# The slot-table reads on GpSimd's queue, and another order for the first half of an attention step

## The chip, the cores and the metric

The kernel runs on one core of one Trainium2 chip. The metric is the device time of one execution in microseconds (us). The engines of the core run side by side, each through its own list of instructions in order: TensorE (PE) multiplies matrices, VectorE (DVE) and ScalarE (ACT) work element by element, GpSimd (POOL) does the same and issues indirect transfers, SyncE (SP) here only issues transfers.

## The reference

The input x is 8 batches x 1024 tokens x 512 channels. Two blocks follow each other, each behind a layer norm and with a residual sum:

```python
theta_q = xh / (1.0 + jnp.abs(w_q)) + b_q + t * phi_q      # theta_k alike, theta_v without t
Q = jnp.concatenate([cos_q, sin_q], axis=-1)               # K alike; V = cos_v + sin_v
scores = jnp.einsum('bqhd,bkhd->bhqk', Q, K) / scale       # 16 heads, 32 + 32 features, causal
out = jnp.einsum('bhqk,bkhd->bqhd', softmax(scores), V)
x = x + cos_o + sin_o                                      # of theta_out = out / (1 + |w_out|) + b_out
...
probs = softmax(x @ Wr + br); topk_p, topk_e = top_k(probs, 2)     # 8 experts, two for each token
buf = rows of x by expert, 160 places for each expert and batch; later tokens are dropped
y = relu(buf @ W1[e] + b1[e]) @ W2[e] + b2[e]                      # 512 -> 2048 -> 512
x = x + sum over both experts of probability * y
```

sin and cos come from a table of 2048 entries with linear interpolation.

## The kernel before, in words

**Attention.** 32 steps, n = 4b + c: batch b, and block c of 128 channels (four heads, two pairs of heads). In one step PE computes, for the first pair, ten tiles of scores (called S1 to S10 here: three for queries 0 to 511, seven for queries 512 to 1023; `scores`, L600 and the mask L614), ACT takes the exponent of each (L620), and PE multiplies each with V (`attend`, L634). The ten products of the first pair are called F1 to F10 here. The second pair has the scores T1 to T10 and products of which only the first three, G1 to G3, are done in the same step; the other seven, R1 to R7, are left for the next step. Products are unlike in width: R7, like F10, has 256 columns, F1 to F3 together have 512 + 512 + 256.

PE's accumulators for scores are three buffers of two banks each (`two_banks`). The same three serve the transposes `turn` (L202, attention output back to tokens), the transposes of `qk_pre`, and the router. A buffer comes free when ACT has taken the exponent, or DVE has copied what it holds.

Between the two halves of a step ACT loads the table of sines, computes the sines for the next step (L514 for the cosine, L433 for the rest) and loads the table of exponents again. DVE multiplies the results (`qk_post`, L436), and eight transfers of SP (L527: four of `qk_c`, four of `qk_r`) rearrange them into the `qk` tiles that the next step's scores read. `qk_f`, `qk_r`, `qk_c` have one buffer each: `qk_pre` of the step after the next writes `qk_r` (L426) only when the L527 transfers have read the old one.

**The order of the work.** On PE, ACT and DVE the order is the order of the program text; it is written out by hand in the loop over n, with generators: `some(k, *gens)` takes k pieces, `with_asides(k)` takes k scores and after each one piece of every side job. The transfers of SP and GpSimd are placed by the tile framework, in an order that it fixes when the program is built; each queue then runs in that order. The first half of a step before the change is, on PE:

R1-R3 | S1-S5 | R4-R6 | S6-S9 | R7 F1 F2 | S10 | `turn` of the step before | F3 | (sines on ACT) F4-F10

and then T1, T2, `turn`, T3-T5, G1-G3, T6-T10, and the transposes of `qk_pre`.

**The router.** When batch b-1 is finished, in the second half of step n = 4b (c = 0), `router` begins: the residual rows go to `out` (L691), then layer norm statistics (L694, L339-L347), normalised rows `xn2` (`rows`, L704) which SP stores for the experts (L710), and four groups of two row tiles. A group has transposes on PE and a copy by DVE to `xT` (`features`, L731; called f0 to f3 here), and logits on PE with copies by DVE to `lg` and `prob` (`sums`, L765, L748, L770, L772; u0 to u4 here, of which u4 only finishes the last group). f0 stands at the end of step c = 0; u0, f1, u1, f2, u2, f3, u3, u4 are dealt out over step c = 1 by `router_step`; the choice of experts follows in c = 2 (`part(route)`), and in c = 3 the slots of the tokens are known. Then `scatter` issues 16 indirect transfers on GpSimd's queue (L682), which write (token, weight) into the batch's slot table in device memory, and `fetch_slots` reads a slot table back into the tile `meta` (L881, two transfers of 8-byte elements, 1280 of them). In the program text of step 4b + 3 the fetch of batch b-2's table stands ahead of the scatters of batch b-1; in SP's queue the framework has put each fetch earlier than that: the reading of a table stands between the `qk_base` load (L476) of the step in which that same table is scattered and the L527 transfers of the step after it.

**Experts.** From L1023 on PE runs the two layers for 8 experts in 16 chunks. `find_rows` and the row gathers L962 need `meta`; the last batch's router runs inside the first chunk (`ending`).

Of the kernel before, what the change touches and what calls it, by code (L numbers as in the profile page):

```python
# [22 lines left out]
B, S, D = 8, 1024, 512  # L23
# [50 lines left out]
def preln_attn_moe_kernel(  # L74
# [21 lines left out]
    nc = tc.nc  # L96
# [404 lines left out]
    def qk_abs(st):  # L501

        f, r = st
        c = qkt.tile([P, 2, S], F32, name="qk_c")
        for i in range(2):
            nc.scalar.activation(c[:, i, :], r[:, i, :], AF.Abs)
            yield c, f, r
        for i in range(2):
            square(f[:, i, :])
            yield c, f, r  # L510
# [26 lines left out]
    def v_pre(n):  # L537

        b, c = divmod(n, NCH)
        t = trig.tile([P, S], F32, name="v_p", bufs=1)  # L540
        p = t.bitcast(I32)
        r = trig.tile([P, S], I32, name="t_r")
        for h in range(2):
            nc.vector.tensor_tensor(
                by_token(t)[:, 4 * h : 4 * h + 4, :],
                xn_tiles[b][h][:, :, c * P : (c + 1) * P], along(inv_v, c, 4), ALU.mult,
            )
        yield p, r
        nc.vector.tensor_tensor(by_token(p), by_token(t), along(bias_v, c), ALU.add)
        yield p, r  # L550
        angle(p, r)
        yield p, r
# [73 lines left out]
    def attend(n, pr, h, es, halves):  # L626

        vt = v_tiles[n % 2]
        av = ps_av.tile([P, 512], F32, name="av")
        tiles = tiles_of(h)  # L630
        for i, parts in enumerate(tiles):
            for kb, q0, w, at in parts:
                for a in range(2):
                    nc.tensor.matmul(  # L634
                        av[a * 64 : (a + 1) * 64, q0 - 512 * h :],
                        lhsT=vt[:, kb, 2 * pr + a, :], rhs=es[i][:, a, at : at + w],
                        start=kb == 0, stop=i + 1 == len(tiles),
                    )
            if i + 1 == len(tiles):
                av_sb = avp.tile([P, 512], F32, name="av_sb")  # L640
                q = 2 * (n % NCH) + pr
                nc.vector.tensor_scalar(av_sb, av, inv_o[:, q : q + 1], None, ALU.mult)
                halves.append(av_sb)
            yield

    def some(count, *gens):

        for gen in gens:
            while count and next(gen, 0) is None:
                count -= 1  # L650

    def rest(gen):
        got = None
        for got in gen:
            pass
        return got
# [207 lines left out]
    def part(gen):  # L864

        for name in gen:
            if name is not None:
                return
            yield

    def keep(box, gen):
        for box[0] in gen:
            yield

    def fetch_slots(b, eng):

        rows = slot_d[b][: E * CAP, :].rearrange("(e c) k -> c e k", e=E)
        s0 = b * CAP
        while s0 < (b + 1) * CAP:
            s1 = min((s0 // P + 1) * P, (b + 1) * CAP)  # L880
            eng.dma_start(  # L881
                meta[s0 % P : s0 % P + s1 - s0, :, s0 // P, :],
                rows[s0 - b * CAP : s1 - b * CAP],
            )
            s0 = s1
# [238 lines left out]
    def experts_begin():  # L1124

        for name, bufs in (("w1p", 3), ("t1p", 2), ("xep", 1), ("tmp_p", 2), ("gp", 2)):
            pools[name] = to_end.pool(name, bufs, **right)
        find_rows(0)
        for k in range(AHEAD):
            load_ahead(k)  # L1130
        yield from start(gather(0), first_parts)
        mix_w1(0, 0)
# [69 lines left out]
    for n in range(NCK):  # L1202
        more, late = n + 1 < NCK, last is not None
        b, c = divmod(n, NCH)
        if n == NCK - 1:
            to_inputs.close()
            first_rows = experts_begin()
        pos_n = trig.tile([P, S], F32, name="o_p")
        if late:
            e11, halves1, pos = last  # L1210
        es, halves = [[], []], [[], []]

        products = [attend(n, 0, h, es[h], halves[0]) for h in range(2)]
        if late:
            products.insert(0, attend(n - 1, 1, 1, e11, halves1))
        ahead = [scores(pairs[0], h, es[h]) for h in range(2)]
        places, v_box = [None], [None]
        absolutes = keep(places, qk_abs(qk_st)) if more else iter(())  # L1220
        asides = [keep(v_box, v_pre(n + 1))] if more else [first_rows]
        if c == 2 and route is not None:
            asides.append(part(route))
        if b == 0 and c in (1, 2):
            asides.append(layernorm1(1, c - 1))
        elif c == 0 and b + 1 < B:
            asides.append(layernorm1(b + 1, 1))
        elif c == 3 and b + 2 < B:
            asides.append(layernorm1(b + 2, 0))

        router_step = lambda: next(route) if c == 1 and route is not None else None

        def with_asides(count):
            for _ in range(count):
                some(1, *ahead)
                for g in asides:
                    next(g, None)

        if late:
            some(3, *products)  # L1240
        router_step()
        if n == 0:
            with_asides(3)
            qk_st = rest(qk_pre(1))
            angle(*qk_st)
            absolutes = keep(places, qk_abs(qk_st))
            with_asides(2)
        else:
            with_asides(5)
        router_step()  # L1250
        some(2, absolutes)
        if late:
            some(3, *products)
        router_step()
        with_asides(4)
        router_step()
        some(2, absolutes)
        if more:
            v_st = v_box[0]
            square(v_st[0])  # L1260
        some(3, *products)
        router_step()
        with_asides(1)
        rest(absolutes)
        for g in asides:
            rest(g)
        if n == 1:
            load_mid(0)
        if late:
            turn(1, halves1, pos)  # L1270
            o_st = o_pre(n - 1, pos)
        router_step()
        if c == 1 and b > 0:
            load_mid(b)
        if n == 2:
            load_b1()
        if c == 2 and b + 2 < B:
            load_x(b + 2)
        if c == 3 and b > 0:
            next(route)  # L1280
            if b > 1:
                fetch_slots(b - 2, nc.sync)
            scatter()


        some(1, *products)
        if more:
            qk_st = places[0]
            qk_sin(qk_st)
            sine(v_st[1])  # L1290
        if late:
            sine(o_st[1])
        if more:
            post = qk_post(qk_st)
            next(post)
        some(NTT, *products)
        if n == 0:
            load_base(2)


        es, halves1 = [[], []], []
        ahead = [scores(pairs[1], h, es[h]) for h in range(2)]
        router_step()
        if c == 2 and route is not None:
            next(route)
        some(2, *ahead)
        turn(0, halves[0], pos_n)
        if more:
            next_pairs = rest(post)
            v_post(n + 1, v_st)  # L1310
        some(3, *ahead)
        if late:
            square(o_st[0])
            o_post(n - 1, o_st)
        some(3, attend(n, 1, 0, es[0], halves1))
        router_step()
        if late and c == 0:
            route = router(b - 1)
            next(route)
        some(5, *ahead)  # L1320
        if n + 2 < NCK:
            qk_st = rest(qk_pre(n + 2))
            angle(*qk_st)
        if late and c == 0:
            next(route)
        if n + 3 < NCK:
            load_base(n + 3)
        last = (es[1], halves1, pos_n)
        pairs = next_pairs if more else None
# [4 lines left out]
    def ending():  # L1334

        o_st = o_pre(NCK - 1, pos_n)
        yield
        sine(o_st[1])
        square(o_st[0])
        for _ in range(3):  # L1340
            yield
        o_post(NCK - 1, o_st)
        for _ in range(3):
            yield
        for name in router(B - 1):

            for _ in range(5 if name == "tiles" else 1):
                yield
        fetch_slots(B - 2, nc.sync)
        scatter()  # L1350
        fetch_slots(B - 1, nc.gpsimd)

    experts(ending())

# [30 lines left out]
```

## Time and profile before

| | us |
|---|---|
| median of 3 runs (lowest, highest) | 3448.29 (3447.84, 3449.66) |
| the profiled execution | 3456.62, its span 3454.9 |
| PE busy / DVE / ACT / POOL in the span | 3239.6 / 2297.2 / 1320.1 / 407.1 |
| first expert product on PE (L1023) starts at | 1430.20 |
| start of the sines (L514), steps 11 to 18 | 531.29, 569.52, 627.91, 667.50, 705.73, 743.96, 801.49, 841.08 |
| mean granted TensorE clock | 0.979 |

The starts of the sines give the length of a step: 38.23 us from one to the next in most places (531.29 to 569.52), 39.6 where the choice of experts runs, and more at the place where the router begins (569.52 to 627.91, 743.96 to 801.49). In a timeline row the columns are start, duration, engine, line, operation, output and inputs, number of instructions merged; the bracket at the end is the idle time before it on that engine and what ended it. A merged group of matmuls is counted to the modelled end of its last one, which overlaps the next group a little, so lengths below are taken from start to start. SPq is SP's queue of transfers: a row there begins when the transfer's waits are over.

### The profile page before, as it was taken

What the parts mean: (1) busy time and instruction counts of PE and PEld (TensorE: products, weight loads), DVE (VectorE), ACT (ScalarE), POOL (GpSimd) and SP (SyncE); (2) the same over time, 40 slices, a digit from 0 to 9 for tenths busy, and PEclk for the clock granted to TensorE, in tenths of its full rate; (3) what the DMA queues carried; (4) which work ended last, traced back from release to release, by engine and by line L of the source; (5) the groups of instructions that cost most, each with busy time, mean ns of one, the idle gap of its engine ahead of it and who ended that gap; (6) DMA issues with size and microseconds to landing.
All of it is one profiled execution on the core that took longest, in us unless ns stands there. A gap on an engine that the chain in (4) does not pass through costs nothing.

```text
span 3454.9 us, 48850 instructions
## 1 busy us (share of the span) xinstructions
PE 3239.6 (94%) x18942; PEld 2177.8 (63%) x18942; DVE 2297.2 (66%) x5064; ACT 1320.1 (38%) x1609; POOL 407.1 (12%) x349
## 2 busy tenths in 40 slices
PE   3999898989898989899999999999999999999998
PEld 1444443444444444468868878778778688688687
DVE  7877777777777767574575576566656746745844
ACT  5777777777777777320111111111101101101201
POOL 1000202020202020331101100100110011011010
PEclk9999999999999999999999999999999999999999
DMA  4534353535263435232322422312322313323321
GB/s 147 142 103 145 90 166 72 165 76 168 73 195 75 147 72 156 68 101 56 113 62 49 113 55 55 107 49 65 109 44 68 107 37 80 101 43 82 95 40 25
DMA packets 242703, 320.79 MB, mean 93 GB/s; under 512 B 30312, under 2 KB 163112, under 8 KB 230056
## 3 DMA queue, kind: packets, MB, share of 16 engines
q1 hardware_dynamic: 220304, 275.54, 27.3%
q0 software_dynamic: 22080, 42.10, 6.8%
q8 instruction: 150, 2.46, 0.3%
q14 instruction: 81, 0.66, 0.1%
q10 hardware_dynamic: 88, 0.02, 0.0%
HBM read 188.67 MB, written 61.82 MB: 73 GB/s over the span
## 4 chain that ended last, share of the span: by engine, by line
PE 74%; ACT 12%; DVE 8%; DMA 3%; issue 2%; SPq 0%; POOL 0%; POOLq 0%; ACTq 0%; DVEq 0%
PE ps_p L1068 28%; PE ps_p L1023 25%; PE ps_s L600 10%; PE av L634 8%; ACT e L620 5%; DMA qk<-qk_r 1%; ACT qk_c L514 1%; ACT qk_f L430 1%; ACT t_r L433 1%; ACT qk_r L433 1%; PE ps_s L202 1%; PE ps_t L979 1%; ACT L620 1%; ACT L514 1%; DVE st_mid L577 1%
## 5 line engine op out<-in xcount | busy, mean ns | idle before, releaser
L620 ACT ACTIVATE e<-ps_s 128x1024 f32<-128x1024 f32 (+1 forms) x640 | 569.4, 937 | 353.3 <-PE ps_s L614 236.4
L600 PE MATMUL ps_s<-qk 64*128 64x512 f32 (+3 forms) x3072 | 612.7, 518 | 67.9 <-ACT e L620 42.2
L1068 PE MATMUL ps_p<-w,hid 128*128 128x256 f32 x2560 | 569.8, 380 | 0.0
L634 PE MATMUL av<-e,v 128*64 128x512 f32 (+3 forms) x3072 | 544.7, 501 | 0.0
L1068 PEld LDWEIGHTS ps_p<-w,hid 128*128 128x128 f32 x2560 | 484.7, 190 | 66.4
L600 PEld LDWEIGHTS ps_s<-qk 64*128 64x128 f32 x3072 | 264.9, 191 | 269.4 <-issue 147.3
L1068 PE MATMUL ps_p<-w_t,hid 128*128 128x256 f32 x1920 | 430.0, 379 | 0.0
L634 PEld LDWEIGHTS av<-e,v 128*64 128x64 f32 x3072 | 205.3, 139 | 320.0 <-issue 305.1
L1068 PEld LDWEIGHTS ps_p<-w_t,hid 128*128 128x128 f32 x1920 | 361.9, 190 | 47.7
L1023 PE MATMUL ps_p<-xe_s,t 128*128 128x256 f32 (+1 forms) x1024 | 299.4, 435 | 5.8 <-DVE t L1008 3.4
L1023 PE MATMUL ps_p<-xe,w 128*128 128x256 f32 (+1 forms) x1024 | 301.2, 437 | 1.3 <-DVE o_p L671 1.2
L1023 PE MATMUL ps_p<-xe,t 128*128 128x256 f32 (+1 forms) x1024 | 296.8, 433 | 0.0
L682 POOL DMA_INDIRECT slot_d<-token,slot x128 | 163.9, 1280 | 1126.8 <-issue 621.6
L1023 PEld LDWEIGHTS ps_p<-xe_s,t 128*128 128x128 f32 x1024 | 194.4, 191 | 90.9 <-DVE t L1008 8.0
L1097 ACT COPY p<-ps_p 128x256 f32<-128x256 f32 x40 | 14.8, 369 | 613.3 <-PE ps_p L1068 613.3
L1023 PEld LDWEIGHTS ps_p<-xe,w 128*128 128x128 f32 x1024 | 194.3, 191 | 84.5 <-DVE hid L1041 5.3
L1023 PEld LDWEIGHTS ps_p<-xe,t 128*128 128x128 f32 x1024 | 194.4, 190 | 80.9 <-issue 0.4
L1090 POOL DMA_INDIRECT out_dram<-y,slots x80 | 126.3, 1578 | 668.2 <-DVE y L1085 531.6
L962 POOL DMA_INDIRECT xg<-xn_d,source x80 | 78.3, 978 | 1053.7 <-PE ps_t L979 1019.2
L1038 ACT ACTIVATE p<-ps_p,b_t 128x256 f32<-128x256 f32 (+1 forms) x128 | 65.5, 511 | 329.7 <-DVE y L1084 169.7
L1042 ACT ACTIVATE hid<-hid 128x256 f32<-128x256 f32 (+1 forms) x128 | 60.1, 470 | 324.6 <-DVE hid L1041 324.6
L1055 ACT ACTIVATE hid<-hid,b_more 128x256 f32<-128x256 f32 (+1 forms) x128 | 71.8, 561 | 277.1 <-DVE hid L1054 277.1
(211 smaller groups left out, 3838.3 us busy)
## 6 DMA issues: line engine op xcount, KB each, us to landing
w<-in_L_ffn_W_dram SPq DMA_DIRECT2D x256, 256.0 KB, 3.3
qk<-qk_c SPq DMA_DIRECT2D x128, 256.0 KB, 4.2
qk<-qk_r SPq DMA_DIRECT2D x128, 256.0 KB, 4.2
w<-in_L_ffn_W_dram SPq DMA_DIRECT2D x64, 512.0 KB, 6.6
qk_base<-base_d SPq DMA_DIRECT2D x29, 1024.0 KB, 5.0
xn_d<-xn SPq DMA_DIRECT2D x72, 256.0 KB, 2.4
x_mid<-in_L_attn_x_dram SPq DMA_DIRECT2D x16, 1024.0 KB, 8.4
out_dram<-x_mid SPq DMA_DIRECT2D x8, 2048.0 KB, 10.1
```

Of the source, the lines that this page charges most:

```text
L433: nc.scalar.activation(r.bitcast(F32), r, AF.Sin, scale=STEP_ACT)
L514: nc.scalar.activation(c, c, AF.Sin, bias=quarter_c, scale=-STEP_ACT)
L600: nc.tensor.matmul(ps[:, a, at : at + w], lhsT=pair[r, 1, kb * P : (kb + 1) * P], rhs=pair[r, 0, q0 : q0 + w], start=at == 0, stop=not own ...
L620: nc.scalar.activation(e, ps[:, :, :n], AF.Exp, scale=UNIT * UNIT / math.sqrt(2 * DH))
L634: nc.tensor.matmul(av[a * 64 : (a + 1) * 64, q0 - 512 * h :], lhsT=vt[:, kb, 2 * pr + a, :], rhs=es[i][:, a, at : at + w], start=kb == 0, ...
L682: nc.gpsimd.indirect_dma_start(out=slot_d[b], out_offset=bass.IndirectOffsetOnAxis(ap=idx, axis=0), in_=src, in_offset=None,)
L962: nc.gpsimd.indirect_dma_start(out=xg, out_offset=None, in_=xn2_d[i % 2], in_offset=bass.IndirectOffsetOnAxis(ap=source[:, e, j0 + j, None ...
L1023: nc.tensor.matmul(ps, lhsT=weights[:, k, :], rhs=rows[:, k, :], start=k == 0, stop=k == 1)
L1038: nc.scalar.activation(p1, product(b11, a11), AF.Identity, bias=b1_t[:, e * NHC + q : e * NHC + q + 1])
L1055: nc.scalar.activation(h12, h12, AF.Relu, bias=more)
L1068: nc.tensor.matmul(ps, lhsT=hs[k][:, part, cols], rhs=ws[k][weight], start=k == 0, stop=k == NHQ - 1,)
L1090: nc.gpsimd.indirect_dma_start(out=out, out_offset=bass.IndirectOffsetOnAxis(ap=meta[:, e, jj[r], 0:1], axis=0), in_=ys[r], in_offset=None ...
```

## The change

Three edits. First, `fetch_slots` issues its two transfers on GpSimd's queue for every batch (before: SP's queue for all batches but the last). As built, GpSimd's queue has each fetch directly behind the 16 scatters that write the same table, and SP's queue has none; the order of SP's other transfers is the same.

Second, the first half of a step is, on PE:

R1-R3 | S1-S5 | R4-R7 | S6-S10 | `turn` of the step before | F1-F3 | (sines on ACT) F4-F10

On ACT the exponent of S10 now comes before the three squarings (L430), not after them.

Third, the router's pieces are dealt out anew: u0, f1, u1 (now behind R7), f2 (behind S10), u2 (ahead of T1), f3 (behind T5), u3 (behind G3); u4 moves into the next step, c = 2, behind R1-R3. Before: u0, f1, u1, f2 (behind S9), u2 (behind F2), f3 (behind `turn`), u3 (ahead of T1), u4 (behind G3).

```diff
-    def fetch_slots(b, eng):
+    def fetch_slots(b):
...
-            eng.dma_start(
+            nc.gpsimd.dma_start(
...
-        if c == 2 and route is not None:
-            asides.append(part(route))
...
         router_step()
+        if c == 2 and route is not None:
+            next(route)
+            asides.append(part(route))
...
         some(2, absolutes)
         if late:
-            some(3, *products)
-        router_step()
-        with_asides(4)
+            some(4, *products)
         router_step()
-        some(2, absolutes)
-        if more:
-            v_st = v_box[0]
-            square(v_st[0])
-        some(3, *products)
+        with_asides(5)
         router_step()
-        with_asides(1)
         rest(absolutes)
         for g in asides:
             rest(g)
+        if more:
+            v_st = v_box[0]
+            square(v_st[0])
...
             o_st = o_pre(n - 1, pos)
-        router_step()
...
-                fetch_slots(b - 2, nc.sync)
+                fetch_slots(b - 2)
...
-        some(1, *products)
+        some(3, *products)
...
         some(3, *ahead)
+        router_step()
         if late:
...
-        fetch_slots(B - 2, nc.sync)
+        fetch_slots(B - 2)
         scatter()
-        fetch_slots(B - 1, nc.gpsimd)
+        fetch_slots(B - 1)
```

More of the change, by code (lines that the diff above doesn't have):

```diff
@@ L1252, in preln_attn_moe_kernel @@
         if late:
-            some(3, *products)
+            some(4, *products)
         router_step()
-        with_asides(4)
+        with_asides(5)
         router_step()
-        some(2, absolutes)
+        rest(absolutes)
+        for g in asides:
+            rest(g)
         if more:
@@ L1260, in preln_attn_moe_kernel @@
             square(v_st[0])
-        some(3, *products)
-        router_step()
-        with_asides(1)
-        rest(absolutes)
-        for g in asides:
-            rest(g)
         if n == 1:
```

## The prediction

> **What bounds the kernel now.** The first part of the page says that PE is 94% busy, so I ask where the other 6% lies, in the sum of PE's waits:
>
> ```profile
> PE ps_s L600 <- ACT e L620: 42.2, 34, 1.8
> PE ps_s L765 <- DVE xT L731: 42.0, 6, 8.2
> PE ps_s L202 <- DVE xn L704: 30.2, 7, 4.5
> PE ps_t L722 <- DVE xn L704: 8.8, 3, 4.4
> ```
>
> (us in all, times, longest.) The first row is one short wait in nearly every step. The second comes six times, 7 us each, at the first logits u0 where a router begins. I followed one of the six back through the timelines of PE, DVE, SPq and POOL:
>
> ```profile
> 780.00 1.08 PE L765 MATMUL ps_s<-xT,wr_sb 128*32 128x256 f32 x8 [7.90 <-DVE xT L731]
> ...
> 777.42 1.23 DVE L426 TENSOR_SCALAR qk_r<-qk_f 128x2048 int32<-128x2048 int32 x1 [7.89 <-DMA qk<-qk_r]
> ...
> 764.41 1.30 SPq L881 DMA_DIRECT2D slots<-slot_d  x2
> 765.82 3.27 SPq L527 DMA_DIRECT2D qk<-qk_c  x4
> 769.18 4.09 SPq L527 DMA_DIRECT2D qk<-qk_r  x4
> ...
> 761.37 0.97 POOL L682 DMA_INDIRECT slot_d<-token,slot  x1 [2.15 <-DMA slot_d<-token,slot]
> ```
>
> u0 waits for DVE's `xT`, which stands behind L426, which waits until the `qk_r` transfers have read their tile. Those are late because SP's queue stood still at L881 until the last scatter (761.37, plus 2 to 3 us to land) was done. Step 4 has a router and no fetch yet, a control inside the trace:
>
> ```profile
> 239.15 3.24 SPq L527 DMA_DIRECT2D qk<-qk_c  x4
> 244.38 3.84 SPq L527 DMA_DIRECT2D qk<-qk_r  x4
> ...
> 260.37 1.23 DVE L426 TENSOR_SCALAR qk_r<-qk_f 128x2048 int32<-128x2048 int32 x1
> 263.12 0.64 PE L765 MATMUL ps_s<-xT,wr_sb 128*32 128x256 f32 x8
> ```
>
> Here the sines began at 234.75 and `qk_c` left 4.4 us later; in step 16 they began at 743.96 and it left 21.9 us later. Last, PE in step 19, an undisturbed one:
>
> ```profile
> 869.26 2.85 PE L600 MATMUL ps_s<-qk 64*128 64x512 f32 x12
> ...
> 873.21 2.38 PE L634 MATMUL av<-e,v 128*64 128x256 f32 x16
> 875.51 0.70 PE L600 MATMUL ps_s<-qk 64*128 64x256 f32 x4
> ...
> 876.72 6.24 PE L634 MATMUL av<-e,v 128*64 128x256 f32 x36
> ...
> 887.39 0.70 PE L600 MATMUL ps_s<-qk 64*128 64x256 f32 x4 [1.71 <-ACT e L620]
> ```
>
> From S6 (869.26) to T3 (887.39), 18.13 us, ACT works without a break (exponents, squarings, table, sines, table, exponent of T1) and PE ends up waiting for it. The other 20 us of a step belong to PE. So work of PE inside this stretch is free up to its 1.7 us of slack, and outside it costs its length.
>
> [...] four ready `qk_c` transfers left 0.1 us after L881. [...] the fetch itself lands in 2.2 to 3.1 us. [...] S1 took 2.08 us behind the wait of 7.90, and 1.13 in step 19.
>
> **Part 1, the fetches.** The lengths from sine start to sine start where a router begins behind a fetch are 54.69, 58.39, 57.53, 58.84, 56.64 and 57.75 us. The control, 234.75 to 282.73, is 47.98. The excesses are 6.71, 10.41, 9.55, 10.86, 8.66 and 9.77, together 55.96 us: 42.0 of waits, and the slow matmuls behind them. What stays in both is PE's wait of 4.4 us for the first normalised rows (L704), since DVE's chain from x_mid is untouched. Gain 56.0.
>
> A seventh scatter (step 31) held SP to 1450.34: L691 (2 MB), two weight loads and the first row stores L710 left then in one bunch. A store then took 6.1 us to land where 2.4 is the median, and PE stood 4.15 us at 1462.97. With SP free the large store leaves when x_mid is ready (1438.6), and this wait goes. Gain 4.2; bounds 0 and 8.
>
> On POOL a fetch waits for the last scatter (1.42 us in the one fetch that is there already) and then issues for 1.60: 3.0 us. Queued behind it is the `token` iota of a router one batch later (about 117 us of idle time cover it), and once, after the seventh scatter, the weight mixing L1007 at 1449.21 whose tile PE first uses about 1469. Cost 0; without that cover it would be 3 us, once.
>
> **Part 2, the order of the first half.** R7 goes from inside ACT's stretch to before it. R7 F1 F2 take 2.30 us (873.21 to 875.51) for 1280 columns, so R7's 256 take 0.46. Moving S10's exponent ahead of the squarings only reorders ACT; F1 and F2 stay in the stretch. Hence +0.46 in each step that ACT bounds: steps 2 to 30 without the seven router steps, 22 x 0.46 = 10.1. Lower bound 0, should ACT's stretch shorten as much; upper bound 1.0, should `turn`, now ahead of F1 and F2, wait for its buffer besides.
>
> **Part 3, the router's pieces.** In the control step 5 the stretch (272.49 to 291.13) is 18.64 us, PE being full there. f3 (16 transposes, 0.55) and one full logit group (287.81 to 288.51, 0.70) leave it for PE's own part: the stretch returns to 18.13, -0.5, and PE's part grows by 1.25, with R7 by 1.71. A new wait comes with it. u3's buffer is free only when DVE has copied `lg` and `prob`, and these copies stand behind L436, L575, the eight L577 and L642 of `o_post` (1.26 + 1.26 + 1.56 + 0.65, start to start). Counted from T3, DVE starts that chain at 4.95 and is done about 10.2; PE, with f3 and u3 between, wants the buffer for T9 about 9.3. That is 0.9, less 0.5 of short waits at the same place now: +0.4. Together 1.6 a router step, x 7 = 11.3. Bounds 0 and 3.5 each.
>
> **Sum.** -56.0 - 4.2 + 10.1 + 11.3 = -38.8 us. Against the profiled execution of 3456.6: 3417.8. The median of the runs shown is 8.3 us lower, so 3448.3 - 38.8 = 3409.5, say 3410. A measurement of this kernel can tell about 0.2%, 7 us.
>
> **Rivals.**
> - *The reordering is free or gains.* For it: PE already waits 1.7 us a step, and fewer changes between kinds of matmul might save a little. Against: that slack lies in ACT's stretch, and R7 is taken out of it. Then 3448.3 - 60 = 3388. Chance 0.17.
> - *The wait moves.* u3's buffer, or rows held by their stores, costs PE 3.5 us or more in each router step (upper bound of part 3) and R7 costs its upper bound: -60 + 22 + 24.5 = -14, so 3435. For it: three buffers shared by scores and router, and DVE's long chain ahead of the copies. Against: the rows' stores are early once SP is free. Chance 0.13.
> - *Slower.* `turn` is now ahead of F1 to F3 in PE's queue and needs S8's buffer and the copy of R7 (L642). If that holds PE until past its slack, F1 to F10 (8.4 us) end after ACT's stretch in every step. It decides from 60/29 = 2.1 us a step; at 2.5 the time is 3448 - 60 + 72 = 3460. Against: in step 19 S8's exponent ends about when S10 would, and R7 is done 4 us before. Chance 0.04.
> - *The stall is not the cause*, and DVE's chain would hold u0 anyway: 3448 + 21 less some, about 3450. Step 4 speaks against it, with the same chain and no wait of that kind. Chance 0.03.
>
> The forecast itself, 3397 to 3424, has 0.63. The range for 8 in 10 takes in the free reordering and part of the moved wait: 3386 to 3431. Faster 0.93, same 0.03, slower 0.04.
>
> **What would show it.** Right: no L881 on SPq; `qk_c` leaves 4 to 5 us after the sines also in steps 8, 12, ... 28; the wait L765 <- xT near 0; sine-to-sine lengths of about 49 where a router begins, and about 38.7 in plain steps, with PE's wait for L620 at T3 about 2.2. In steps c = 1 a wait of about 1 us at T9 for DVE's `prob`. The wait at L722 in the first expert chunk halved. The forecast is wrong if plain steps stay at 38.2 or below, if they exceed 39.3, or if L426 still waits for `qk_r`.

## The result: 3436 us, a third of the forecast gain

| | before | after |
|---|---|---|
| median of 8 runs each (lowest, highest) | 3447.58 (3443.57, 3449.66) | 3435.97 (3433.86, 3437.27) |
| profiled execution, its span | 3456.62, 3454.9 | 3435.24, 3433.3 |
| first L1023 on PE starts at | 1430.20 | 1417.1 |
| sines of step 0 to sines of step 30 | 1289.10 | 1275.15 |

The ratio is 0.9967, with a 95% interval from 0.9956 to 0.9978: 11.6 us gained where 38.8 were forecast (3410, range 3386 to 3431). The profiled execution of the kernel before is 9 us above its median, that of the changed one 0.7 below, so the medians give the gain in all and the traces say where in the steps it lies.

**What came as forecast.** The stalls are gone. From the sum of PE's waits in the changed kernel (us in all, times, longest):

```profile
PE ps_s L600 <- ACT e L620: 61.6, 41, 2.5
PE ps_s L202 <- DVE xn L704: 30.1, 7, 4.7
...
PE ps_p L1023 <- POOL t L1008: 4.1, 2, 3.6
PE ps_s L600 <- DVE prob L772: 3.7, 7, 0.5
...
PE ps_t L722 <- DVE xn L704: 2.6, 2, 2.3
...
PE ps_s L765 <- DVE xT L731: 0.9, 2, 0.7
```

The wait for `xT` fell from 42.0 to 0.9 us, L722 from 8.8 to 2.6; L704 stayed at 30. The start of the router in step 16, from the timelines of SPq, POOL, DVE and PE of the changed kernel; the sines begin at 747.79:

```profile
752.18 3.25 SPq L527 DMA_DIRECT2D qk<-qk_c  x4
756.63 3.23 SPq L527 DMA_DIRECT2D qk<-qk_r  x4
...
764.00 1.55 POOL L881 DMA_DIRECT2D slots<-slot_d  x2 [2.16 <-DMA slot_d<-token,slot]
...
774.66 1.23 DVE L426 TENSOR_SCALAR qk_r<-qk_f 128x2048 int32<-128x2048 int32 x1
...
777.95 0.64 PE L765 MATMUL ps_s<-xT,wr_sb 128*32 128x256 f32 x8
```

`qk_c` leaves 4.4 us after the sines (before: 21.9), the fetch stands on POOL, and L426 and u0 wait for nothing.

**What did not.** The first row of the waits: 61.6 us where 42.2 were, and, worse, what follows such a wait. The forecast had plain steps of 38.7 us; plain lengths are those from the sines of a step c = 2 or c = 3 to the next sines, with no start of a router and no choice of experts in them. In the changed kernel some are 38.66, and others 40.3. Here is T3 to T5 on PE in one of each, steps 18 and 19:

```profile
847.32 0.70 PE L600 MATMUL ps_s<-qk 64*128 64x256 f32 x4 [1.60 <-ACT e L620]
...
848.24 1.99 PE L600 MATMUL ps_s<-qk 64*128 64x512 f32 x8
...
867.85 2.85 PE L600 MATMUL ps_s<-qk 64*128 64x512 f32 x12
...
872.82 7.96 PE L634 MATMUL av<-e,v 128*64 128x512 f32 x48
...
885.99 0.70 PE L600 MATMUL ps_s<-qk 64*128 64x256 f32 x4 [2.49 <-ACT e L620]
...
886.90 3.68 PE L600 MATMUL ps_s<-qk 64*128 64x512 f32 x8
```

The same eight matmuls of T4 and T5 take 1.99 us in step 18 and 3.68 in step 19. ACT, which takes the exponents of these scores, waits for them in step 19:

```profile
888.93 1.02 ACT L620 ACTIVATE e<-ps_s 128x1024 f32<-128x1024 f32 x1 [1.52 <-PE ps_s L600]
```

A second wait of 0.68 us follows; in step 18 there is one of 0.67 alone. So the next sines come about 1.65 us later. T4 and T5 that take 2.9 us or more are called halved below. Of steps 2 to 29, 13 have them after the change (2, 3, 6, 8, 10, 12, 15, 16, 19, 20, 23, 26, 27; step 30 too, whose length is not shown here), and two before it (3 and 24). That is 11 x 1.65 = 18 us. The granted TensorE clock, 0.50 behind the wait of 2.49 us, explains the 3.68. The changes of the granted clock in this trace, 46 between 60 and 1420 us, lie 3.413 us or a multiple of it apart, and this view gives busy time in stretches cut on that grid, around step 7 (T3 behind a wait of 2.48, but T4 and T5 in 1.99) and around step 19; columns: stretch, length, busy PE, PEld, DVE, ACT, POOL, then the granted clock, DMA share, GB/s:

```profile
371.62:375.03 3.41, 2.23 (x36) 1.50 (x32) 2.73 (x5) 3.39 (x4) 1.81 (x1) 1.00 0.44 82
375.03:378.44 3.41, 1.97 (x14) 1.19 (x16) 3.18 (x2) 2.73 (x5) 1.60 (x1) 1.00 1.01 231
378.44:381.86 3.42, 3.42 (x22) 1.29 (x20) 0.42 (x1) 2.96 (x3) 0.57 (x1) 1.00 0.98 238
880.21:883.62 3.41, 3.29 (x44) 1.93 (x39) 2.76 (x3) 3.39 (x4) 2.53 (x1) 1.00 0.19 36
883.62:887.03 3.41, 0.91 (x10) 0.63 (x12) 3.38 (x4) 3.40 (x4) 1.13 (x1) 1.00 0.95 205
887.03:890.44 3.41, 3.41 (x8) 0.98 (x8) 0.83 (x1) 1.40 (x2) 0.53 (x1) 0.50 0.98 229
```

In step 19 the wait of 2.49 us falls inside one stretch; PE is busy for 0.91 of its 3.41 us, and the whole next stretch runs at clock 0.50. In step 7 the boundary at 375.03 cuts the wait in two; PE is busy 2.23 and 1.97 us, and the clock stays at 1.00.

The wait itself grew by more than R7. From S6 (867.85) to the end of the transposes ahead of T3 (T3's start less its wait), PE takes 15.7 us in the changed step 19 and 16.4 in the old one; 0.44 of the difference is R7, and the other 0.3 is time that PE saves in the new order, which has two changes between products (L634) and other matmuls fewer there. PE gains nothing by it, since it then waits for ACT that much longer.

### The profile page after: what moved, and what is told of

Same layout as the page of the kernel before. It is cut to its first block, busy times and chain, and to the rows that moved or that the text cites. A ratio compares the mean times of both kernels' runs of the same rounds, so it can differ in the third digit from the quotient of the medians.

```text
span 3433.3 us, 48857 instructions
## 1 busy us (share of the span) xinstructions
PE 3238.3 (94%) x18942; PEld 2176.1 (63%) x18942; DVE 2292.8 (67%) x5064; ACT 1319.5 (38%) x1609; POOL 411.8 (12%) x363
## 4 chain that ended last, share of the span: by engine, by line
PE 76%; ACT 14%; DVE 7%; DMA 1%; issue 1%; POOL 0%; POOLq 0%; SPq 0%; DVEq 0%; ACTq 0%
PE ps_p L1068 28%; PE ps_p L1023 25%; PE ps_s L600 12%; PE av L634 7%; ACT e L620 3%; ACT qk_f L430 2%; ACT qk_c L514 2%; ACT t_r L433 2%; ACT qk_r L433 2%; PE ps_s L202 1%; ACT L620 1%; ACT L514 1%; PE ps_t L979 1%; ACT v_p L430 1%; PE ps_s L614 1%
## 5 line engine op out<-in xcount | busy, mean ns | idle before, releaser
L600 PE MATMUL ps_s<-qk 64*128 64x512 f32 (+3 forms) x3072 | 616.3, 520 | 91.7 <-ACT e L620 61.6
L634 PE MATMUL av<-e,v 128*64 128x512 f32 (+3 forms) x3072 | 541.3, 503 | 0.0
L634 PEld LDWEIGHTS av<-e,v 128*64 128x64 f32 x3072 | 204.9, 140 | 317.0 <-issue 306.7
L1023 PE MATMUL ps_p<-xe_s,t 128*128 128x256 f32 (+1 forms) x1024 | 299.2, 435 | 7.5 <-POOL t L1008 4.1
L1023 PE MATMUL ps_p<-xe,w 128*128 128x256 f32 (+1 forms) x1024 | 300.5, 437 | 1.5 <-DVE o_p L671 1.2
L1023 PE MATMUL ps_p<-xe,t 128*128 128x256 f32 (+1 forms) x1024 | 296.8, 433 | 0.0
L1023 PEld LDWEIGHTS ps_p<-xe_s,t 128*128 128x128 f32 x1024 | 194.4, 191 | 92.6 <-DVE t L1008 7.9
L1023 PEld LDWEIGHTS ps_p<-xe,w 128*128 128x128 f32 x1024 | 194.0, 191 | 84.5 <-DVE hid L1041 5.7
L1023 PEld LDWEIGHTS ps_p<-xe,t 128*128 128x128 f32 x1024 | 194.4, 190 | 80.9 <-issue 0.4
```

Of the source, the lines that this page charges most:

```text
L600: nc.tensor.matmul(ps[:, a, at : at + w], lhsT=pair[r, 1, kb * P : (kb + 1) * P], rhs=pair[r, 0, q0 : q0 + w], start=at == 0, stop=not own ...
L634: nc.tensor.matmul(av[a * 64 : (a + 1) * 64, q0 - 512 * h :], lhsT=vt[:, kb, 2 * pr + a, :], rhs=es[i][:, a, at : at + w], start=kb == 0, ...
L1023: nc.tensor.matmul(ps, lhsT=weights[:, k, :], rhs=rows[:, k, :], start=k == 0, stop=k == 1)
```

## The experiments

Two theories for the missing gain: the *clock theory* (PE's longer wait at T3 halves the clock for T4 and T5), and that the *order* or the *fetch* costs more than forecast in the ordinary way (a wait, a buffer, a queue). Times are medians and ratios are to the kernel before, run on the same chip: runs 1 to 4, 5 to 8 and 9 to 11 used three chips, with medians of 3449.7, 3447.8 and 3452.1 for the kernel before. So a difference between runs of two groups is good to some 4 us. In some expectations the clock theory is called that of half windows: the window is the 3.413 us between the places of the 46 changes of clock, and the half stands for PE's busy share in it, which was 0.49 or less in all 23 full-clock stretches of the changed kernel that a halved one followed (begun from 70 to 1420 us).

### 1. The fetch alone

```diff
-                fetch_slots(b - 2, nc.sync)
+                fetch_slots(b - 2, nc.gpsimd)
...
-        fetch_slots(B - 2, nc.sync)
+        fetch_slots(B - 2, nc.gpsimd)
```

> The order of the kernel before and its router pieces, with the fetches alone moved to GpSimd's queue. Both theories on the lost gain agree that the stalls are gone here. If the fetch move is worth what the prediction gave it (56 us in the router steps, 4 to 8 at the start of the experts), the time is 3448 - 60 to 64 = 3384 to 3388, plain steps stay at 38.2 us, PE's wait for L620 at T3 stays at 1.71 us and T4, T5 stay at full clock in nearly all steps. If instead the fetch on GpSimd gives back part of its gain somewhere (a rival for the missing 26 us), the time is 3400 to 3415.

Measured: 3394.7 us, 0.9849 (0.9831 to 0.9867) of before. So the fetch is worth 55 us and the rest of the change takes some 41 back (0.9967 against 0.9849). Sines of step 0 to 30: 1235.45, 53.65 less than before; plain steps 38.23, of steps 2 to 29 only 3 and 24 have halved T4 and T5. Of the 4 to 8 us at the start of the experts little came: behind the sines of step 30 the profiled execution is 1.5 us shorter than before. PE's waits at L722 fell from 8.8 to 2.3 us, as forecast, but two new ones stand there, 1.90 us at L765 and 3.80 for the weight mixing (timelines of POOL and PE of this run):

```profile
1404.44 0.97 POOL L682 DMA_INDIRECT slot_d<-token,slot  x1 [3.22 <-DMA slot_d<-token,slot]
1406.87 1.57 POOL L881 DMA_DIRECT2D slots<-slot_d  x2 [1.46 <-DMA slot_d<-token,slot]
1408.46 0.73 POOL L1007 TENSOR_TENSOR t<-w 128x256 f32<-128x256 f32 x1
...
1409.82 0.72 POOL L1008 TENSOR_TENSOR t<-w,t 128x256 f32<-128x256 f32 x1
...
1410.60 2.92 PE L1023 MATMUL ps_p<-xe_s,t 128*128 128x384 f32 x4 [3.80 <-POOL t L1008]
```

The mixing L1007 stands behind the last scatter in POOL's queue, but the fetch waits for that scatter to land and issues ahead of it: 1.46 + 1.57 = 3.0 us, and PE, 53 us earlier than before at this point, stands 3.80 us for the result. In the changed kernel PE arrives later, and this wait is 0.50; the 3.6 in the sum of its waits above is a later one for another L1008, which was 2.42 before the change.

### 2. The order and the router pieces alone

The changed kernel with `fetch_slots(b - 2, nc.sync)` and `fetch_slots(B - 2, nc.sync)` as before.

> The changed order and router pieces, with the fetches still on SP's queue. Clock theory (PE's longer wait at T3 makes the clock drop to one half for T4 and T5): R7 22 x 0.46 = 10, router 7 x 1.85 = 13, slow T4 and T5 in about 11 more steps x 1.65 = 18, together +41, so 3489 (3480 to 3497), with plain steps of both 38.7 and 40.3 us. If the order costs only what the prediction gave it (21 us) and the missing gain is the fetch's, 3469.

Measured: 3473.6, 1.0070 (1.0054 to 1.0085). Thirteen steps from 2 to 29 have halved T4 and T5, with the fetch where it was before: they belong to the order. The total misses the 3489 because the stall is smaller here: PE's wait for `xT` (L731) is 19.4 us, not 42.0. In step 16 the fetch leaves SP's queue 16.3 us after the sines in place of 20.5 (the 16 scatters keep their own pace, 53.0 us from the start of the first to that of the last in the kernel before and 52.7 here, while the step around them has become longer). So the two edits do not add up: with the stall there, part of the order's cost is hidden in it.

### 3. The wait filled

```diff
         turn(0, halves[0], pos_n)
+        if more and not (c == 1 and b > 0):
+            spare = ps_av.tile([P, 512], F32, name="av")
+            nc.tensor.matmul(spare, lhsT=ident, rhs=halves[0][1], start=True, stop=True)
+            nc.tensor.matmul(
+                spare[:, :256], lhsT=ident, rhs=halves[0][1][:, :256], start=True, stop=True
+            )
```

> The changed kernel with two matmuls more in each step that has the wait (all but the router steps): products of the identity with an attention tile, 128x512 and 128x256 columns, about 1.3 us, into an accumulator that nobody reads, between the transposes of turn and T3. Clock theory: the wait falls from 2.49 to about 1.2 us, T4 and T5 take 1.99 us from start to modelled end in all steps, plain steps are all 38.66, and the time falls by 12 to 13 x 1.65 = 20 to 3416 (3413 to 3420), though PE has more to do. Rival (the 40.3 us steps come from the order, a buffer or a transfer): the filling changes nothing, 3436, or adds its length, 3436 + 22 x 1.3 = 3465.

Measured: 3423.0, 0.9924 (0.9909 to 0.9940): 13 us less than the changed kernel, with more work on PE. Its PE in step 19:

```profile
870.74 1.13 PE L1306 MATMUL av<-av_sb,ident 128*128 128x512 f32 x2
871.71 0.59 PE L1307 MATMUL av<-av_sb,ident 128*128 128x256 f32 x2
873.30 0.70 PE L600 MATMUL ps_s<-qk 64*128 64x256 f32 x4 [1.00 <-ACT e L620]
...
874.22 1.99 PE L600 MATMUL ps_s<-qk 64*128 64x512 f32 x8
```

T4 and T5 are 1.99 us in every step and all plain steps 38.66: the order itself costs 0.43 a step, and the rest was the clock. From sines 0 to sines 30 it is 1256.75, 18.4 less than the changed kernel, as expected; some of it is lost at the start of the experts, where PE now waits 4.15 us for L1008 at the place seen in run 1 (0.50 in the changed kernel).

### 4. R7 back inside, behind S9, and 6. behind S10

Run 4: R4-R6 | S6-S9 | R7 | S10 | `turn` | F1-F3. Run 6: R4-R6 | S6-S10 | R7 F1 F2 | `turn` | F3. Both from the changed kernel; the diff is run 4's.

```diff
-            some(4, *products)
+            some(3, *products)
         router_step()
-        with_asides(5)
+        with_asides(4)
+        if late:
+            some(1, *products)
+        with_asides(1)
```

> The changed kernel with R7 put back behind S9, into ACT's stretch; F1 to F3 stay behind turn and the router pieces as changed. The step of the prediction for R7: plain steps at full clock shorten by 0.46, from 38.66 to 38.2, 22 x 0.46 = 10 us. Clock theory besides: the wait at T3 falls from 2.49 to about 2.0, so that fewer steps have slow T4 and T5, perhaps 6 of 15 in place of 10: 5 to 8 us more. Together 3418 to 3421. Rival (the wait at T3 has no part in it): 3426.

> The changed kernel with R7 F1 F2 behind S10 and ahead of turn, so that S10's exponent still precedes the squarings but R7 is inside ACT's stretch and delays no score of the first pair. If R7's 0.46 us in PE's own part is what makes a full-clock step 38.66 in place of 38.23, these steps are 38.2 here, with a wait at T3 near 2.0. Theory of half windows [...]: a wait of 2.0 us still hits 2.0 / 3.41 = 0.59 of the 14 plain steps in place of 0.73, so 3436 - 10 - 2 = 3424 (3418 to 3430). If the 0.43 us has another cause than R7, the full-clock steps stay at 38.6 to 38.7 and the time at 3432 to 3438.

Measured: run 4 3437.4 (3424.7 to 3442.1; ratio 0.9963, 0.9949 to 0.9977), run 6 3434.8 (3418.2 to 3435.6; 0.9950, 0.9934 to 0.9966). Both miss the hoped gain (3418 to 3421, and 3424). Run 6 shows the reason in part: S6 begins 28.18 us after the sines, as in run 1 (28.62 in the changed kernel), so R7's 0.44 is real; but its full-clock steps are 38.42, because ACT takes 0.2 us longer: the exponent of S6 starts 29.41 after the sines in both, the next sines come at 38.42 (run 1: 38.23). A likely cause is that S10's exponent, which now stands ahead of the squarings, writes one of the two `e_256` buffers, which R7 has to read first; no row shows it, so this is not shown. In run 4 ACT waits 0.28 us for S10's scores behind R7, and steps are 38.62. The waits at T3, mostly 1.69 and 1.96, still halve the clock in 7 of 14 steps each (the steps c = 3 and c = 0). The wide spread of the runs fits a number of halved places that differs between executions.

### 5 and 8. More products inside: R6, then R5 and R6

Both from run 1; the diff is run 5's. Run 8 has 1 and 5 in place of 2 and 4.

```diff
         if late:
-            some(3, *products)
+            some(2, *products)
         router_step()
         with_asides(4)
...
-        some(3, *products)
+        some(4 if late else 3, *products)
```

> e1_fetch_only with R6 moved from ahead of S6 to ahead of R7, so that R6 R7 F1 F2 stand behind S9. This is the prediction's reading of the two parts of a step turned round: 0.91 us (a third of the 2.73 us of R4 to R6) leaves PE's own part and goes into the wait. ACT idles 0.83 us ahead of the exponent of S6 now, so at most 0.83 can be won: plain steps 38.23 - 0.83 = 37.4, the wait at T3 about 0.9 in place of 1.71, no slow T4 and T5 after step 0. 22 x 0.83 = 18 and two slow places less, 3: 3395 - 20 = 3374 (3371 to 3380). If the prediction's reading is wrong and the position of products costs in another way, 3395 or more.

> e5_r6_inside with R5 moved as well (R4 alone is left ahead of S6). ACT has no idle time left ahead of S6's exponent, so nothing more is to be won there; PE then has 1.8 us more in the stretch than e1_fetch_only, about as much as the wait of 1.71. Equal to e5_r6_inside within 5 us if the stretch holds it, 5 to 20 us slower if S10 or turn comes late for ACT.

Measured: 3411.4 (0.9895, 0.9881 to 0.9909) and 3428.2 (0.9948, 0.9935 to 0.9961): slower than run 1 by 17 and 33 us, where run 5 was forecast to be 20 faster. My reading that PE's work is free inside ACT's stretch was incomplete. From the sum of ACT's waits of run 5, and its ACT in step 19:

```profile
ACT e L620 <- PE av L634: 35.8, 31, 1.5
```

```profile
852.81 1.03 ACT L620 ACTIVATE e<-ps_s 128x1024 f32<-128x1024 f32 x1 [1.05 <-PE av L634]
```

This wait is not among run 1's. S9's exponent writes the `e` buffer that R6 still has to read (`e_512` has 8 buffers), so R6 behind S9 holds ACT itself, 1.05 us a step. That is more than the 0.87 us by which the exponent of S6 comes earlier (28.55 us after the sines, 29.41 in run 1). Full-clock steps are 38.39 (38.81 in run 8), with waits at T3 of 1.86 and 1.91 and 5 and 10 halved places.

### 7. The router pieces alone, and 11. R7 alone

Run 1 with one of the other two edits each. Run 7:

```diff
-        if c == 2 and route is not None:
-            asides.append(part(route))
...
+        if c == 2 and route is not None:
+            next(route)
+            asides.append(part(route))
...
         with_asides(4)
-        router_step()
         some(2, absolutes)
...
         some(3, *products)
-        router_step()
         with_asides(1)
+        router_step()
...
             o_st = o_pre(n - 1, pos)
-        router_step()
...
         some(3, *ahead)
+        router_step()
```

> e1_fetch_only with the router pieces dealt out as in the change (u4 in step c = 2, and so on), but R7 F1 F2 S10 in the old order. Part 3 of the prediction alone: 7 x 1.6 = 11.3, or 7 x 1.85 = 13 by the steps of the changed kernel's trace: 3395 + 11 to 13 = 3406 to 3408, plain steps 38.23, no more than two slow T4 and T5. Rival (the deal costs only together with the changed order): 3395 to 3399.

Measured: 3418.2 (0.9915, 0.9903 to 0.9928), so +23.5. The lengths from sines to sines behind c = 1 are 41.34 in place of 39.58: 7 x 1.76 = 12.3, the size expected (forecast 11.3). Besides, five places are halved (7, 11, 15, 19, 27) in place of two, 3 x 1.65 = 5, at the very same wait of 1.71 us: other step lengths put the wait at another place against the boundaries, as shown in the last section. These two make up the 18 us by which steps 0 to 30 are longer in the traces; the other 5 us of the medians are not placed.

Run 11:

```diff
-            some(3, *products)
+            some(4, *products)
         router_step()
         with_asides(4)
...
-        some(3, *products)
+        some(2 if late else 3, *products)
```

> e1_fetch_only with R7 alone moved, from behind S9 to behind R6 and so out of ACT's stretch; S10, turn, F1 to F3 and the router pieces as before. Part 2 of the prediction by itself: full-clock plain steps 38.66 (+0.44), the wait at T3 1.71 + 0.44 = 2.15 us. The prediction stopped there: 3395 + 22 x 0.44 = 3405. Theory of half windows: a wait of 2.15 us leaves PE less than half busy in 2.15 / 3.41 = 0.63 of the places where it can lie, so of 14 plain steps about 9 have slow T4 and T5 and 40.3 us, against 2 in e1_fetch_only: 3405 + 7 x 1.65 = 3416 (3408 to 3424; the phase decides, and it can hold from batch to batch).

Measured: 3416.5 (0.9895, 0.9880 to 0.9911), so +21.8 where the prediction's step allows 10. The wait at T3 is 2.14 us, full-clock steps are 38.66, those behind c = 1 39.82 (+0.24), and 7 of 14 places are halved: 3, 8, 12, 16, 20, 23, 28. That is 14 x 0.43 + 7 x 0.24 + 5 x 1.65 = 16 us, of 17.0 that steps 0 to 30 are longer in the traces.

### 9 and 10. A squaring of ACT moved into its idle time

One piece of `absolutes` more ahead of S6's exponent, in run 1 (run 9) and in the changed kernel (run 10):

```diff
-        some(2, absolutes)
+        some(3, absolutes)
         if late:
```

> e1_fetch_only with the first of the two squarings of qk_f (L430, 1.09 us) on ACT ahead of the exponent of S6 in place of behind that of S9. There ACT idles 0.83 us in e1_fetch_only, until PE has done R4 to R6; no tile of e is held longer than before, which is what the runs e5 and e8 seem to have failed on. ACT's stretch behind S6 shortens by 1.09 - 0.26 = 0.83: plain steps 37.4, the wait at T3 about 0.9, so under half a window, and no slow T4 and T5 after step 0. 22 x 0.83 + 2 x 1.65 = 21: 3395 - 21 = 3374 (3370 to 3380). If ACT's idle time there is not what sets a step, 3395.

> The changed kernel with the same one move of a squaring on ACT. ACT idles 1.26 us there, so all of the 1.09 us is won in ACT's stretch: full-clock plain steps 38.66 - 1.09 = 37.6, the wait at T3 2.49 - 1.09 = 1.4 us, below half of a window of 3.41 us. Theory of half windows: no slow T4 and T5 (13 x 1.65 = 21 us) on top of 22 x 1.09 = 24: 3436 - 45 = 3391 (3385 to 3400). If the slow T4 and T5 do not come from the length of the wait, they stay, and the time is 3412.

Measured: 3369.7 (0.9773, 0.9760 to 0.9787) and 3390.1 (0.9827, 0.9814 to 0.9840). Run 9 beats both kernels, the changed one by 66 us. ACT and PE of run 9 in step 19:

```profile
827.93 1.15 ACT L430 ACTIVATE qk_f<-qk_f,split_c 128x1024 f32<-128x1024 uint16 x1
828.97 3.81 ACT L620 ACTIVATE e<-ps_s 128x1024 f32<-128x1024 f32 x4
...
844.77 0.70 PE L600 MATMUL ps_s<-qk 64*128 64x256 f32 x4 [0.70 <-ACT e L620]
...
845.69 1.99 PE L600 MATMUL ps_s<-qk 64*128 64x512 f32 x8
```

ACT has no idle time ahead of S6's exponent (0.83 in run 1), the wait at T3 is 0.70, plain steps are 37.23, and no step has halved T4 and T5. Run 10 is the sharper test of the clock theory, since its PE order is that of the changed kernel. Its PE in step 19:

```profile
854.46 0.70 PE L600 MATMUL ps_s<-qk 64*128 64x256 f32 x4 [1.45 <-ACT e L620]
...
855.38 1.99 PE L600 MATMUL ps_s<-qk 64*128 64x512 f32 x8
```

The wait is 1.45 us, none of the 13 places is left, plain steps are 37.62, and the time is the 3391 of the clock theory, not 3412.

### The waits side by side

Places are the steps c = 3 and c = 0 from 3 to 28, 14 in each kernel:

| wait at T3, us | kernel | places with halved T4, T5 |
|---|---|---|
| 0.70 | run 9 | 0 |
| 1.00 | run 3 | 0 |
| 1.45 | run 10 | 0 |
| 1.71 | before, run 1, run 7 | 2, 2, 5 |
| 1.86, 1.91, 1.96 | runs 5, 8, 6 | 5, 10, 7 |
| 2.14 | run 11 | 7 |
| 2.49 | changed, run 2 | 9, 8 |

Run 4 has other, short waits of PE beside the 1.69 and is left out of the table. So are the steps c = 2, where the wait is shorter: 1.60 us in the changed kernel and in runs 2, 4, 6 and 11, with 0.1 us of short gaps beside it (0.4 in the first two). In the six such steps from 6 to 26 it was followed by halved T4 and T5 in 3, 4, 4, 3 and 0. So 1.60 to 1.71 is an edge, not a safe length.

## Why the prediction was wrong, point by point

**The step that failed** is in part 2: "F1 and F2 stay in the stretch. Hence +0.46 in each step that ACT bounds". The 0.44 us is right (S6 begins 28.62 after the sines, not 28.18), and so is the next link, PE's longer wait at T3 (2.2 forecast, 2.49 measured). But I priced a wait that ACT sets at nothing, since ACT is the one that is late. It costs 1.65 us where it halves the clock for the scores behind it, and ACT then waits for these scores. I had even seen S1 at 2.08 us behind the wait of 7.90, against 1.13 in step 19, but used it only for waits of that size. The upper bound of 1.0 a step was about another cause (`turn` waiting for its buffer), which came to 0.16 us in each of seven router steps.

The forecast against steps 0 to 30 of the traces (from sines to sines):

| term, us | forecast | measured | by |
|---|---|---|---|
| stalls behind the fetch | -56.0 | -53.65 | run 1 against before |
| R7 and router pieces at full clock | +21.4 | 14 x 0.43 + 7 x 1.85 = +19.0 | changed kernel against run 1 |
| halved T4 and T5 | 0 | 11 x 1.65 = +18.2 | changed kernel against run 1 |
| steps 0 and 1, and the lengths where a router begins | 0 | +1.1, +1.3 | changed kernel against run 1 |
| sum | -34.6 | -14.1; the traces differ by -13.95 | |
| start of the experts | -4.2 | -1.5 | run 1 against before |

In this account the halved T4 and T5 are the term that was left out. The counts are those of one execution each, and they differ between executions. Behind step 30 the profiled changed kernel is 7.7 us shorter than the one before, 6.2 of it in the waits at L722; the rest is not placed, and in the medians the whole gain is 11.6.

- *Part 1*: the mechanism was right, and the size nearly so (56.0 forecast, 53.65 measured); the 4.2 at the start of the experts was not to be had in full. "Cost 0; without that cover it would be 3 us, once" names the place; the cover, PE needing the tile 20 us later, goes when PE comes early. Runs 1 and 3 show it.
- *Part 2*: beside the clock, the 0.46 was counted in 22 steps. As 0.43 it came in the 14 steps c = 3 and c = 0; in the steps c = 2 it is part of the 1.85 below (0.24 in run 11, which moves R7 alone). The reading behind it, that ACT works without a break from S6 on, left out that ACT stands idle for 0.83 us until S6's scores are there, the gap that run 9 fills.
- *Part 3*: right in size. 1.76 a router step (run 7), 1.85 with R7, for 1.6. The new wait at T9 for DVE's `prob` is there, 0.53 us where about 0.9 was forecast.
- *Rivals*: the time is that of "the wait moves" (3435), but by chance: its cause, u3's buffer, costs 0.53 and not 3.5. The true mechanism was none of the four.
- *What would show it*: the sign that I had set down, plain steps over 39.3, is the one that came, in 9 of 14 steps c = 2 and c = 3.

## What to carry to other kernels

That another engine was the late one did not make a wait of TensorE free slack here (1.65 us where the clock was halved behind it): look at what the matmuls behind it cost, in the granted clock and in one group's duration from step to step. In these traces the waits that cost something were those of 1.6 us and longer, about half of the 3.413 us between the places where the clock changed; filling one (run 3) or shortening it (runs 9 and 10) took the cost away. Here one squaring of 1.09 us, moved from ACT's full stretch into ACT's idle time, gave 25 us on the fetch alone and 46 on the changed order. Before moving work into another engine's shadow, ask what it holds there: R6 held a buffer that ACT wanted next.

## What the runs showed of the hardware

All 46 changes of the granted clock in the changed kernel's trace between 60 and 1420 us lie at 2.98 us + k x 3.4133 us, within 0.03; in the kernel before they lie at 3.02 us + k x 3.4133 us. The traces of six kernels (before, changed, runs 1, 3, 4 and 11) were cut at such places, each at its own, into stretches that begin from 70 to 1420 us. Of the full-clock stretches in which PE was busy for less than 47%, 83 of 86 are followed by a halved one; of those above 53%, 1 of 2112; in between 14 of 22. The two limits were chosen on these same traces. In the changed kernel PE was busy for 0.35 of the stretch in the median of the 23 that a halved one followed (0.27 at the wait of step 19), and for none of it in only two.

So in these runs it counts where a wait lies. In the kernel before and in runs 1 and 7, all with a wait of 1.71 us, its middle stands 0.76 to 1.22 us behind a boundary in all nine halved places, and in none of the 33 others. From the 3.413 us and the counts around one half I estimate that a wait of w us between 1.7 and 3.4 leaves a stretch less than half busy in about w of 3.41 positions: 0.73 for 2.49 us (9 and 8 of 14 measured) and 0.63 for 2.14 (7 of 14). The positions are not independent: a batch takes 167.2 us in run 7 and 167.1 in most of run 11, which is 49.0 of these stretches, so a place that is hit is hit again, in run 7 in five steps c = 3 and in run 11 in five steps c = 0.

On SP and on POOL, what stood behind a fetch left when the fetch had been issued: in the kernel before the four ready `qk_c` transfers 0.11 us after it (764.41 + 1.30 to 765.82), in run 1 L1007 0.02 us after it (1406.87 + 1.57 to 1408.46). The fetch's 3.0 us (1.46 of wait, 1.57 of issue) did not vanish with the move; it stands in another queue, and showed as soon as PE came for what is behind it: PE stood 3.80 us at L1023.
